# Softmax division moved behind the value product, with the sums broadcast by way of DRAM and the order laid out anew

## The chip, the cores and the metric

The kernel runs on one core of a Trainium2 chip. Its time is in device microseconds (us). A core has a matmul engine (PE, with its weight loads shown apart as PEld), a vector engine (DVE), an activation engine (ACT), a general engine (POOL, GpSimd) and a queue that only issues DMAs here (SP). Each takes its instructions in order; they wait for one another by semaphores. SBUF is the memory on the core, PSUM the matmuls' output memory (used here as two buffers of 128 x 1024 floats and four of 128 x 512), DRAM the memory outside.

## The reference

One transformer layer on x of shape (2, 1024, 512): attention with 16 heads of 32, then a feed-forward part with signs of weights, each followed by a residual and a layer norm. Everything is float32.

```python
qkv = jnp.einsum('bsd,ed->bse', x, w_qkv) + b_qkv          # (2, 1024, 1536)
q, k, v = ...                                              # (2, 16, 1024, 32)
scores = jnp.einsum('bhqd,bhkd->bhqk', q, k) / math.sqrt(Hd)
scores = scores + causal
attn = jax.nn.softmax(scores, axis=-1)
out = jnp.einsum('bhqk,bhkd->bhqd', attn, v)
...
x = layernorm(x + out @ w_out.T + b_out)
hidden = relu((x @ sign(up_weight).T) * up_scale)          # 2048 wide
x = layernorm(x + (hidden @ sign(down_weight).T) * down_scale * output_scale)
```

The softmax divides each row of exps by its sum. The sum depends on the query alone, so the division can be made on the probabilities or on the row of the value product.

## The kernel before

The attention runs in eight chunks: for each batch b (2) and each group e of four heads (4). A chunk has eight query tiles i of 128 rows; tile i needs the keys of i + 1 blocks of 128. For each chunk, `project` makes q, k and v of the four heads. To keep float32 accuracy in a faster matmul type, x and the weights are cut into forms (`prepare`: L585 truncates, L597 subtracts, L603 scales, L610 or L618 subtract again), and `matmuls` (L664) multiplies the forms. q and k are split once more (`split`, L746 and L751, on POOL) and written to DRAM and read back as "stacks", four loads for each (`stack`, DMAs of SP). x of batch 1 is loaded and cut in `load_x` (eight tiles), weights in `load_w` (three for a chunk).

`attend` handles a query tile. `scores` (L984, or L964 in the first half of the first chunk) makes scores of one, two or four heads in one of two double PSUM buffers ("d"). DVE adds the mask and takes the negated row maximum (L1021, or L1003 and L1013 where four heads go together), ACT takes the exp and sums each row (L1036, with the sums beside it in "small"). DVE takes the reciprocal of the sums (L1048), and POOL multiplies each row of probabilities by it (L1054, one instruction for each head). `transposes` (L1083) turns the probabilities block by block into a PSUM bank, and DVE or ACT copies them to SBUF (L547 is ACT's, L549 DVE's, `copied`). `values` (L1110) multiplies v by the turned probabilities; the result for a tile, four heads of 32 on the partitions and 128 queries along the row, is copied to "atT". When the last group of a batch is done, `output` (L1169) multiplies by the output weights, adds the residual and takes the layer norm's moments. The feed-forward part (L1296, L1340) runs at the end, from about 500 us on.

The order of the work is not that of the Python loops. Every step is a `Task` with a place (a number that grows with the work; one chunk is 36 units, as it has 36 blocks), the engines that may do it with a cost on each, and the tiles it reads and writes. `Plan.schedule` walks a clock of its own over these costs and gives, for each engine, the ripe task with the lowest place; where a task lists two engines, the one free first takes it. The result is a fixed order on each engine. Tiles have few slots, so a task can also wait for a buffer. A DMA counts as landed 2.3 units of that clock and its size over 200 GB/s after it is issued.

Lists at the top of the file shift places chunk by chunk: `LO` and `HI` bound the stretch over which the next chunk's projection is paced, `LOADW` and `PREPW` (and `LOADX`, `PREPX` for x of the second batch) say how far ahead of the chunk's base its weights are loaded and cut, `EAGER` how far the score matmuls go ahead, `FAST` the copies from PSUM, `BACK` the value product, `WAIT` the split of q and k, `TILES` the order of a chunk's query tiles, `TOGETHER` the tiles whose value product is held back and made with the next one, `ORDER` the order of the six products of a projection.

Probabilities live in a ring "pr" of four times 1024 columns, turned ones in "pt".

Of the kernel before, what the change touches and what calls it, by code (L numbers as in the profile page):

```python
# [11 lines left out]
F32R = mybir.dt.float32r  # L12
# [17 lines left out]

FAST = [8, 10, 8, 8, 8, 2, 8, 0]


TOGETHER = [(1, 3, 5), (1, 3, 5), (0, 1, 3, 5), (0, 3, 5), (0, 1, 3, 4, 6), (0, 1, 3), (0, 2, 4, 6), ()]
TILES = [[0, 1, 2, 3, 4, 5, 6, 7], [0, 1, 2, 3, 4, 5, 6, 7], [0, 1, 2, 3, 4, 5, 6, 7], [0, 1, 2, 3, 4, 5, 6, 7], [3, 2, 1, 0, 7, 6, 5, 4], [0, 1, 2, 4, 3, 5, 6, 7], [1, 2, 3, 0, 4, 5, 7, 6], [0, 1, 2, 3, 4, 5, 6, 7]]
HURRY = 6.0
# [3 lines left out]

HI = [0.9, 0.95, 0.95, 0.9, 0.8, 0.85, 0.95, 0.8]
LO = [0, -2, -4, 3, -1, -2, -2, -4]
LOADW = [15, 30, 30, 20, 5, 30, 30, 20]
LOADX = 10
PREPW = [2, 12, 10, 18, -6, 6, 18, 22]
PREPX = -5
BACK = [1, 1, 1, 4, 1, 9, 1, 1]
ORDER = [3, 0, 0, 0, 0, 0, 4, 4]
WAIT = [0, 8, -4, -2, 2, -2, 0, 4]
ONESX = (-6, 2, 4, 2)  # L50
# [8 lines left out]
SHARES = {'tp': 2, 'po': 1, 'f': 3, 'pu': 3, 'pb': 1}  # L59
EAGER = [25, 25, 20, 20, 20, 20, 20, 20]  # L60
WARM = 9
# [241 lines left out]
def kernel(  # L303
# [89 lines left out]
    def place_for(stack, name, n, kind=F32, side="left"):  # L393
# [5 lines left out]
    a_h = place_for(right, "split", 2 * 2 * TB, side="right")  # L399
    a_fl = place_for(right, "tmp", 3 * TB, side="right")  # L400
    a_v, a_wo, a_xb, a_at = (
        area("v", 2 * NQ * P), area("wout", NC * D), area("rows", 2 * D), area("atT", NC * S)
# [3 lines left out]
    def scratch(name, shape):  # L406
        return dram.tile(shape, F32, tag=name, name=name)

    d_x, d_w = scratch("dx", [NC, P, S]), scratch("dw", [NC, P, 3 * D])
    d_y = [scratch(f"dy{k}", [P, D]) for k in range(B * NQ)]  # L410
    d_h = [scratch(f"dh{k}", [2, P, TB]) for k in range(B * NC * 4)]
# [7 lines left out]

    a_pr, a_pt = place_for(left, "probs", 4 * 2 * TB), place_for(left, "probsT", PTB * P)  # L420

# [12 lines left out]
        "dy": d_y,  # L434
        "dh": d_h,
        "bqk": [bqk],
        "atT": views(a_at, (NC, P)),
# [58 lines left out]
    def of(t):  # L496
# [6 lines left out]
    rings = {  # L503
        "pr": (a_pr, 4 * 2 * TB // P), "pt": (a_pt, PTB)
    }
# [66 lines left out]

    latest = {}
    biases, dx, dw = new("bqk"), new("dx"), new("dw")

    def prepare(t, part, scaled, place, raw=None, parts=None):

        at = slice(None) if scaled else part
        flat = (lambda a: a.rearrange("p (a b) -> p a b", a=NC)) if scaled else (lambda a: a)
        form = lambda k: of(t)[:, k, at]  # L580
        T, given = new("tmp"), raw or (lambda: form(0).bitcast(F32))
        parts = parts or [t[0, part]]
        plan.task(
            dve(0.43),
            lambda _: nc.vector.tensor_scalar(  # L585
                flat(of(T)).bitcast(I32), given().bitcast(I32), -4096, None, ALU.bitwise_and
            ),
            place, parts, [T[0]], label="trunc",
        )
        if raw:  # L590
            plan.task(
                act(0.59), lambda _: nc.scalar.copy(form(0), flat(of(T))), place, [T[0]],
                [t[0, part]], label="high",
            )
        plan.task(
            either(0.69, 1.264),
            lambda e: engine[e].tensor_tensor(form(1), given(), flat(of(T)), ALU.subtract),  # L597
            place, [*parts, T[0]], [t[1, part]], label="low",
        )
        if scaled:  # L600
            plan.task(
                act(0.59),
                lambda _: nc.scalar.activation(  # L603
                    form(1), form(1).bitcast(F32), AF.Copy, scale=1 / U
                ),
                place, updates=[t[1, part]], label="scaled",
            )
            plan.task(
                either(0.69, 1.264),
                lambda e: engine[e].tensor_tensor(  # L610
                    form(2), flat(of(T)), form(1).bitcast(F32), ALU.subtract
                ),
                place, [T[0], t[1, part]], [t[2, part]], label="differ",
            )
        else:
            plan.task(
                dve(0.69),
                lambda _: nc.vector.scalar_tensor_tensor(  # L618
                    form(2), form(1).bitcast(F32), -1 / U, of(T), ALU.mult, ALU.add
                ),  # L620
                place, [T[0], t[1, part]], [t[2, part]], label="differ",
            )
# [119 lines left out]
    def split(hl, place, src=None, parts=()):  # L742

        hi, given = (lambda: of(hl)[:, 0]), src or (lambda: of(hl)[:, 1])
        plan.task(
            pool(0.61), lambda _: nc.gpsimd.tensor_copy(hi().bitcast(F32R), given()), place,  # L746
            parts or [hl[1]], [hl[0]], label="hi",
        )
        plan.task(
            pool(1.264),  # L750
            lambda _: nc.gpsimd.tensor_tensor(of(hl)[:, 1], given(), hi(), ALU.subtract),  # L751
            place, [*parts, hl[0]], updates=[hl[1]], label="lo",
        )
        return hl
# [31 lines left out]
    def project(b, e, lo, hi):  # L786

        v, got = new("v"), {}
        place = pace(lo, hi, 2 * (3 * 3 * NC + 2))
        for n, h in ORDERS[ORDER[b * NC + e]]:  # L790
            if n < 2:
                hl = split(product(b, e, n, h, place), place() - WAIT[b * NC + e])
                got[n, h] = stack(hl, n, place() - WAIT[b * NC + e])
            else:
                values_of(b, e, v, h, place)
        made[b, e] = got, v
# [152 lines left out]

    def scores(b, e, i, heads, at):  # L950
        G, N, W = len(heads), (i + 1) * P, 2 * TB // len(heads)
# [4 lines left out]

        sc, nm, sums = new("sc"), new("nm"), new("sums")
        pr = new("pr", blocks=G * (i + 1))
# [74 lines left out]
        for j in range(G):  # L1033
            marks[b, e, i] = plan.task(
                {"ACT": (0.25 + 0.852 * N / 1000, 0.37 + 0.852 * N / 1000)},
                lambda _, j=j: nc.scalar.activation(  # L1036
                    keys(of(pr), j, N),
                    keys(of(sc), j, W),
                    AF.Exp,
                    bias=of(nm)[:, j : j + 1],  # L1040
                    scale=sign,
                    accum_out=of(sums)[:, j : j + 1],
                ),
                at, [*[sc[1, k] for k in range(G)], nm[j]], [pr[j], sums[0]], label="exp",
            )
        plan.task(
            dve(0.16),
            lambda _: nc.vector.reciprocal(of(sums)[:, :G], of(sums)[:, :G]),  # L1048
            at - 50, updates=[sums[0]], label="recip",
        )  # L1050
        for j in range(G):
            plan.task(
                pool(0.254 + 0.843 * N / 1000),
                lambda _, j=j: nc.gpsimd.tensor_scalar(  # L1054
                    of(pr)[:, j * N : (j + 1) * N],
                    of(pr)[:, j * N : (j + 1) * N],
                    of(sums)[:, j : j + 1],
                    1.0,
                    ALU.mult,
                    ALU.mult,  # L1060
                ),
                at, [sums[0]], updates=[pr[j]], label="norm",
            )
# [34 lines left out]
    def values(b, e, some, at):  # L1098
# [27 lines left out]
        for n, (i, _) in enumerate(some):  # L1126
# [4 lines left out]
                at - FAST[b * NC + e], [to[0]], [rows[e]], label="at",  # L1131
            )

    waiting, marks = [], {}

    def attend(b, e, i, base, hold_back):

        units = grouped(i, 2 if (b, e) in plain and i < NQ // 2 else 4)
        each = []
        for n, heads in enumerate(units):  # L1140
            at = base + (i + 1) * n / len(units)
            pr = scores(b, e, i, heads, at)
            pt = transposes(i, heads, pr, at)
            each += [(u, pt, j * (i + 1)) for j, u in enumerate(heads)]
        waiting.append((i, each))
        if not hold_back:
# [7 lines left out]
    def output(b, i, place):  # L1154
# [7 lines left out]
        plan.task(  # L1162
            pool(1.264), lambda _: nc.gpsimd.tensor_tensor(of(xb), of(xb), bo, ALU.add), place(),
            [wout["bo"]], updates=[xb[0]], label="xb",
# [110 lines left out]
    def feed_forward(up, dn, dsc, base):  # L1275
        UNIT = 2.0

        def block(tb):
# [9 lines left out]
            for f in range(NFC):  # L1288
                pu, hf = new("pu"), new("hf", right_side)
                hh, hr = new("hh", ["pr", "pt"]), new("hr", ["pr", "pt"])  # L1290
                at = start + f * UNIT - (HURRY if final else 0)
# [139 lines left out]
    for at, (b, e) in enumerate(chunks):  # L1431
# [37 lines left out]
        if at + 1 == len(chunks):  # L1469
# [17 lines left out]
            for tb in range(1, NT // TB):  # L1487
                at0 = ff + (tb - 1) * NFC * 2.0
                load_rows(tb, at0 + 4)
                turn(tb, pace(at0 + 12, at0 + 28, 16), ["pr", "pt"])  # L1490
            feed_forward(up, dn, dsc, ff)
# [55 lines left out]
```

## Time and profile before

| | us |
|---|---|
| median of 3 runs (lowest, highest) | 761.28 (760.85, 761.53) |
| the profiled execution | 760.95 |
| its span, first to last instruction | 759.2 |
| PE busy | 735.4 |
| DVE busy | 533.3 |
| ACT busy | 415.5 |
| POOL busy | 333.0 |

The first two groups of the profile's costliest ones and the DMA queues (busy time and mean ns of one; packets, megabytes and share of 16 engines' span):

| group | |
|---|---|
| L1054 POOL, probabilities times reciprocal, x256 | 197.6 us, 782 ns |
| L1036 ACT, exp, x256 | 190.4 us, 754 ns |
| L1021 DVE, mask and maximum, x200 | 173.6 us, 876 ns |
| first DMA queue | 62,352 packets, 90.79 MB, 42.7% |
| second DMA queue | 1,232 packets, 0.53 MB, 0.2% |

A busy engine is one that has an instruction in flight. PE's matmuls overlap, so a busy PE need not be at its peak, but an idle one is lost time if PE sets the end. The profile can also be cut into stretches, which tells at what time each engine stood idle; and for each idle time it names the instruction that ended it. The granted clock is the share of full speed that PE was given in a stretch; it is 0.995 over the span.

### The profile page before, as it was taken

Reading aid. Unit: us, or ns where it says so; the run is one execution under the profiler, and the core shown is the slowest. Engines: PE = TensorE matmul, PEld = TensorE weight load, DVE = VectorE, ACT = ScalarE, POOL = GpSimd, SP = SyncE. Lnnn points to the kernel's source line nnn. Section 1 sums busy time; section 2 is a strip of 40 time slices with the busy share of each in tenths; the row PEclk is TensorE's granted clock in tenths of the full one; section 3 lists DMA queues with packets and bytes.
Section 4 is the critical chain, followed back from the end, with each engine's and each line's share of the span. In section 5 each row is a group of like instructions: output and inputs, shape, how many; then the busy total and the mean of one; then the engine's idle time right before and its main releaser. Section 6 shows DMA issues by size and latency. Waiting matters only on the chain.

```text
span 759.2 us, 15510 instructions
## 1 busy us (share of the span) xinstructions
PE 735.4 (97%) x5778; PEld 578.0 (76%) x5778; DVE 533.3 (70%) x1224; ACT 415.5 (55%) x934; POOL 333.0 (44%) x385
## 2 busy tenths in 40 slices
PE   9979999999879999999999999999999999999996
PEld 4657778888747777788888876667787777878885
DVE  5878977898998676697898789844337337335636
ACT  3637868788627467587788878734222222222210
POOL 2746675776874666567578565511001002001000
PEclk9999999999999999999999999999999999999998
DMA  7759965765716464474364384563003003000101
GB/s 218 174 137 274 241 200 141 164 186 132 200 71 152 136 158 132 106 194 132 94 154 137 90 266 140 175 210 113 1 0 111 1 0 112 1 0 1 56 0 57
DMA packets 63659, 92.32 MB, mean 122 GB/s; under 512 B 5088, under 2 KB 23648, under 8 KB 63584
## 3 DMA queue, kind: packets, MB, share of 16 engines
q1 hardware_dynamic: 62352, 90.79, 42.7%
q8 instruction: 46, 0.75, 0.4%
q10 hardware_dynamic: 1232, 0.53, 0.2%
q14 instruction: 29, 0.24, 0.1%
HBM read 66.66 MB, written 29.88 MB: 127 GB/s over the span
## 4 chain that ended last, share of the span: by engine, by line
PE 86%; DVE 9%; POOL 2%; issue 2%; ACT 1%; DMA 1%; ACTq 0%; DVEq 0%; POOLq 0%
PE s L1083 15%; PE s L1296 15%; PE pd L1340 14%; PE s L664 13%; PE d L984 9%; PE s L1110 8%; PE s L1169 7%; DVE d L1021 1%; DVE xforms L618 1%; POOL probs L1054 1%; PE s L914 1%; PE s L1245 1%; PE s L873 1%; PE s L705 1%; DVE small L1386 1%
## 5 line engine op out<-in xcount | busy, mean ns | idle before, releaser
L1054 POOL TENSOR_SCALAR probs<-probs,small 128x128 f32<-128x128 f32 (+7 forms) x256 | 197.6, 782 | 116.1 <-DVE small L1048 86.2
L1036 ACT ACTIVATE probs<-d,small 128x128 f32<-128x128 f32 (+7 forms) x256 | 190.4, 754 | 46.3 <-DVE small L1021 28.0
L1021 DVE CUSTOM_DVE_ANT_0 d<-d,mask 128x384 f32<-128x384 f32 (+7 forms) x200 | 173.6, 876 | 27.1 <-PE d L984 22.1
L1083 PE MATMUL s<-ident,probs 128*128 128x128 f32 x1152 | 169.0, 274 | 5.7 <-ACT probsT L547 2.4
L664 PE MATMUL s<-xforms,wforms 128*128 128x512 f32 x504 | 165.7, 431 | 2.0 <-DVE xforms L618 0.9
L1083 PEld LDWEIGHTS s<-ident,probs 128*128 128x128 f32 x1152 | 135.3, 141 | 37.7 <-issue 12.5
L1340 PE MATMUL pd<-stacks,hid 128*128 128x512 f32 (+1 forms) x512 | 132.9, 393 | 0.6 <-DVE hid L1313 0.6
L1296 PE MATMUL s<-xt,up 128*128 128x512 f32 x512 | 133.5, 400 | 0.0
L547 ACT COPY probsT<-s 128x512 f32<-128x512 f32 (+3 forms) x204 | 101.8, 528 | 52.8 <-PE s L1083 48.4
L1307 ACT ACTIVATE hf<-s,ups 128x512 f32<-128x512 f32 x64 | 44.0, 688 | 154.2 <-PE s L1296 146.5
L1313 DVE CAST hid<-hf 128x512 fp32r<-128x512 f32 x64 | 28.1, 438 | 124.7 <-ACT hf L1307 124.6
L984 PE MATMUL d<-stacks 128*128 128x512 f32 (+2 forms) x368 | 107.2, 382 | 6.1 <-ACT probs L1036 6.1
L1296 PEld LDWEIGHTS s<-xt,up 128*128 128x128 f32 x512 | 94.3, 188 | 23.8 <-issue 1.4
L1340 PEld LDWEIGHTS pd<-stacks,hid 128*128 128x128 f32 x512 | 92.9, 188 | 23.4 <-DVE hid L1313 1.5
L664 PEld LDWEIGHTS s<-xforms,wforms 128*128 128x128 f32 x504 | 87.0, 189 | 20.7 <-issue 6.1
L549 DVE COPY probsT<-s 128x512 f32<-128x512 f32 (+3 forms) x142 | 81.5, 582 | 14.2 <-PE s L1083 9.9
L1378 POOL TENSOR_TENSOR atT<-atT,back 128x512 f32<-128x512 f32 x9 | 12.9, 1449 | 166.5 <-issue 101.3
L984 PEld LDWEIGHTS d<-stacks 128*128 128x128 f32 x368 | 59.3, 190 | 27.0 <-ACT probs L1036 13.5
L1110 PE MATMUL s<-probsT,v 128*32 128x128 f32 x2304 | 72.1, 274 | 0.0
L1110 PEld LDWEIGHTS s<-probsT,v 128*32 128x32 f32 x2304 | 60.4, 110 | 14.6 <-issue 5.5
L1169 PE MATMUL s<-wout,atT 128*128 128x512 f32 x128 | 65.5, 603 | 0.0
L1036 ACT ACTIVATION_READ_ACCUMULATOR probs<-d,small 128x1 f32 x256 | 54.1, 211 | 0.0
(91 smaller groups left out, 671.0 us busy)
## 6 DMA issues: line engine op xcount, KB each, us to landing
stacks<-dh SPq DMA_DIRECT2D x124, 256.0 KB, 5.4
dh<-split SPq DMA_DIRECT2D x31, 512.0 KB, 3.3
wforms<-dw SPq DMA_DIRECT2D x18, 256.0 KB, 3.6
rows<-in_x SPq DMA_DIRECT2D x16, 256.0 KB, 4.4
dy<-rows SPq DMA_DIRECT2D x16, 256.0 KB, 2.2
raw<-in_up_wT SPq DMA_DIRECT2D x4, 1024.0 KB, 5.1
back<-dy SPq DMA_DIRECT2D x16, 256.0 KB, 4.6
out<-atT SPq DMA_DIRECT2D x16, 256.0 KB, 2.0
```

The source lines that it names most:

```text
L547: nc.scalar.copy(dst, src)
L549: nc.vector.tensor_copy(dst, src)
L664: lambda _, k=k, m=m, c=c: nc.tensor.matmul(bank(ps), lhsT=of(w)[:, m, c], rhs=of(x)[:, m, c], start=(k == 0), stop=(k + 1 == NC * len(for ...
L984: nc.tensor.matmul(of(sc)[:, at0 : at0 + n], lhsT=of(st[0, h])[:, u, ts(z, P)], rhs=of(st[1, g])[:, u, :n], start=True, stop=True,)
L1021: lambda _, j=j, some=some: nc.vector.tensor_tensor_reduce(some(), some(), keys(mask[:, S - N :], 0, N), scale=-1.0, scalar=LARGEST, op0=A ...
L1036: lambda _, j=j: nc.scalar.activation(keys(of(pr), j, N), keys(of(sc), j, W), AF.Exp, bias=of(nm)[:, j : j + 1], scale=sign, accum_out=of( ...
L1054: lambda _, j=j: nc.gpsimd.tensor_scalar(of(pr)[:, j * N : (j + 1) * N], of(pr)[:, j * N : (j + 1) * N], of(sums)[:, j : j + 1], 1.0, ALU. ...
L1083: lambda _, k=k, c=c, tp=tp: nc.tensor.transpose(of(tp)[:, k, :], of(pr)[:, c], ident),
L1110: nc.tensor.matmul(of(to)[ts(u, HD), n, :], lhsT=of(v)[:, k, ts(u, HD)], rhs=turned(pt, c + k, 1)[0], start=(k == i), stop=(k == 0),)
L1169: lambda _, c=c: nc.tensor.matmul(bank(py), lhsT=of(a)[:, c, :], rhs=of(wout)[:, c, :], start=(c == 0), stop=(c == NC - 1),),
L1296: lambda _, f=f, c=c, n=n, pu=pu: nc.tensor.matmul(of(pu), lhsT=of(up)[:, f // TPB, c, ts(f % TPB, P)], rhs=of(xt)[:, n, c, :], start=(c = ...
L1340: lambda _: nc.tensor.matmul(of(to)[:, d0:d1], lhsT=of(h)[:, ts(t, P)], rhs=of(dn)[:, f // 4, f % 4, d0:d1], start=(f == 0 and n == 0), st ...
```

## The change

The probabilities stay undivided through the transposes and the value product. One tile "sums" (128 queries by four heads) now serves all heads of a query tile; its reciprocal is taken once, written to DRAM as four rows of 128, and read back so that each of the four heads' 32 partitions holds its row of 128 reciprocals. POOL multiplies the tile of "atT" by that.

```diff
-        plan.task(
-            dve(0.16),
-            lambda _: nc.vector.reciprocal(of(sums)[:, :G], of(sums)[:, :G]),
-            at - 50, updates=[sums[0]], label="recip",
-        )
-        for j in range(G):
-            plan.task(
-                pool(0.254 + 0.843 * N / 1000),
-                lambda _, j=j: nc.gpsimd.tensor_scalar(
-                    of(pr)[:, j * N : (j + 1) * N],
...
-                at, [sums[0]], updates=[pr[j]], label="norm",
-            )
         return pr
...
                 at - FAST[b * NC + e], [to[0]], [rows[e]], label="at",
             )
+            plan.task(
+                pool(0.48),
+                lambda _, rows=rows, part=shares[b, e, i]: nc.gpsimd.tensor_tensor(
+                    of(rows)[:, e, :], of(rows)[:, e, :], of(part), ALU.mult
+                ),
+                at - FAST[b * NC + e], [shares[b, e, i][0]], updates=[rows[e]], label="share",
+            )
...
+        plan.task(
+            dve(0.16), lambda _: nc.vector.reciprocal(of(sums), of(sums)), at - 50,
+            updates=[sums[0]], label="recip",
+        )
+        line, shares[b, e, i] = new("dr"), new("rb")
+        dma(at - 40, lambda: of(line).rearrange("u q -> q u"), lambda: of(sums), 64,
+            [sums[0]], [line[0]], label="sums")
+        dma(
+            at - 40, lambda: of(shares[b, e, i]),
+            lambda: of(line).rearrange("(u o) q -> u o q", o=1).to_broadcast([NU, HD, P]), 64,
+            [line[0]], [shares[b, e, i][0]], label="shares",
+        )
```

Room for eight of these broadcast tiles ("rb") is taken from the probabilities' ring, which goes from four to three times 1024 columns; 64 small DRAM tiles ("dr") are new.

The costs that the planner uses for the cuts and splits change (for example truncation 0.43 to 0.60, subtraction on DVE 0.69 to 0.95 and on POOL 1.264 to 1.32). The lists of shifts change too, and one is new: `SKEW` shifts the three products of the second half of a projection to later places.

```diff
-FAST = [8, 10, 8, 8, 8, 2, 8, 0]
+FAST = [4, 8, 14, 8, 10, 8, 8, 6]
...
-LO = [0, -2, -4, 3, -1, -2, -2, -4]
-LOADW = [15, 30, 30, 20, 5, 30, 30, 20]
-LOADX = 10
-PREPW = [2, 12, 10, 18, -6, 6, 18, 22]
-PREPX = -5
-BACK = [1, 1, 1, 4, 1, 9, 1, 1]
-ORDER = [3, 0, 0, 0, 0, 0, 4, 4]
-WAIT = [0, 8, -4, -2, 2, -2, 0, 4]
...
+LO = [0, -3, 3, 13, -1, 1, 0, 13]
+LOADW = [30, 20, 10, 30, 15, 5, 15, 20]
+LOADX = 0
+PREPW = [0, 6, 10, 12, 8, 2, 0, 12]
+PREPX = 8
+SKEW = [16, 0, 0, 6, 0, 0, 4, 20]
+BACK = [0, 14, 1, 2, 14, 6, 0, 4]
+ORDER = [3, 0, 0, 0, 2, 0, 4, 4]
+WAIT = [8, -4, -4, 0, -2, -8, 2, -8]
...
+        whole, late = place, SKEW[b * NC + e]
         for n, h in ORDERS[ORDER[b * NC + e]]:
+            place = lambda units=0, h=h: whole(units) + h * late
```

`HI`, `TOGETHER`, `TILES` and `EAGER` change in the same way; the tile order 3, 2, 1, 0, 7, 6, 5, 4 goes from the fifth chunk to the fourth.

## The prediction

> **What bounds the kernel now.** I read the stretches first, then the waits, then the chain that ended last inside the worst stretch. Of the stretches (columns: microseconds from the span's start, length, then busy time and instruction count of PE, its weight loads, DVE, ACT and POOL, granted clock, DMA share, GB/s):
>
> ```profile
> 20.00:60.00 40.00, 35.05 (x266) 25.72 (x265) 31.85 (x62) 19.99 (x48) 23.37 (x24) 1.00 0.66 168
> 60.00:120.00 60.00, 57.51 (x607) 46.63 (x610) 51.82 (x131) 47.59 (x118) 41.62 (x51) 1.00 0.80 222
> 180.00:240.00 60.00, 53.26 (x514) 40.61 (x516) 55.14 (x119) 36.20 (x90) 44.39 (x46) 0.97 0.59 154
> 240.00:300.00 60.00, 60.00 (x511) 44.31 (x502) 43.46 (x99) 38.03 (x92) 38.15 (x43) 1.00 0.49 134
> 740.00:759.20 19.20, 12.90 (x67) 10.63 (x66) 12.69 (x31) 1.87 (x5) 0.00 (x0) 0.89 0.15 56
> ```
>
> PE is the bound: 735.4 of 759.2 us. Its 23.8 us of idle time stand in few places: 1.8 at the start, 4.95 in 20 to 60, 2.5 in 60 to 120, 6.7 in 180 to 240, 6.3 after the last matmul, and 1.6 in all the rest. So 14.2 us are open to a change of attention; from 240 on nothing is. In the worst stretch DVE is busy 55.14 of 60 us, and the clock falls to 0.97, which makes 53.26 us of PE work some 1.6 us longer. Open in all: 15.8 us.
>
> Who waits for whom (total, times, longest), of PE, its loads and POOL:
>
> ```profile
> PE d L984 <- ACT probs L1036: 6.1, 6, 3.6
> PE s L1083 <- POOL probs L1054: 1.4, 1, 1.4
> PEld s L1083 <- POOL probs L1054: 7.4, 19, 1.6
> POOL probs L1054 <- DVE small L1048: 86.2, 72, 4.2
> ```
>
> The transposes seldom wait for the normalising multiply on POOL (1.4 us that reached PE; 7.4 on loads, mostly under running matmuls). PE waits more for score buffers that the exps have not freed. The chain shows who made those late (start, length, what):
>
> ```profile
> 205.33 1.99 POOL probs L1054 x2
> ...
> 212.86 2.36 POOL xforms L597
> ...
> 215.24 1.28 DVE xforms L618
> ...
> 216.92 2.78 DVE xforms L618 x2
> ...
> 221.30 1.57 DVE xforms L597
> ```
>
> This is batch 1's x being cut into its forms (eight tiles, L585, L597, L618) in one burst on DVE and POOL, while the row maxima (L1021) and so the exps stand behind it in DVE's queue. DVE is slowed there, as the view of one line shows (min/median/max ns).
>
> ```profile
> L618 DVE SCALAR_TENSOR_TENSOR xforms<-xforms,tmp x16: 673/692/1767, 5.8 to 223.4; 128x512 fp32r<-128x512 f32 x16
> ```
>
> The same operation takes 673 or 1767 ns; POOL's instructions run beside the long ones.
>
> **Part by part.** Counts are those of the instructions in the two programs; PE has the same 4491, in another order, so its work does not change.
>
> *Removed on POOL:* 256 multiplies (L1054), 197.6 us. *Added on POOL:* 64 multiplies of 128x128 by the broadcast reciprocals. No such row exists: the nearest are the multiply by a column at 128x128 (0.388 us) and the two-tensor add at 128x512 (L1163, 1.305). Scaling the second by the first kind's ratio 0.388/0.804 gives 0.63, nearer the lower; 64 of them 40 us (25 to 84). Five "low" subtractions also come over from DVE, 5 x 1.3 = 6.5 us. POOL goes from 333 to about 182 us.
>
> *DVE:* 64 reciprocals instead of 178, 114 x 0.159 = 18.1 us less; 15 fewer 128x512 copies of transposed probabilities, 15 x 0.686 = 10.3 (ACT takes them, 15 x 0.591 = 8.9, inside its 45% idle); five fewer subtractions, 5 x 0.95 = 4.8. The lengthening beside POOL is, over L585, L597, L610 and L618, the busy time less count times shortest: 4.6 + 5.3 + 3.4 + 4.9 = 18.2 us; it could lose all or none, and as POOL's attention work halves I take 9. Together DVE loses 33 to 51, I take 42 of 533 us. Nothing of this is on PE's path by itself: it shortens what PE's 14.2 idle microseconds wait for.
>
> *Chain from exp to transposes:* a reciprocal (0.16) and a multiply (0.39 to 1.18) less. The matmuls of other work cover this today, so it is worth 1.4 us, and that lies inside the terms below.
>
> *Moved:* the split of batch 1's x is placed 13 units of the order earlier (PREPX -5 to 8) and the projection that needs it 10 later (LO of that chunk 3 to 13). Its eight loads on SP come 10 units later (LOADX 10 to 0, at the chunk's base), so the split can't start before the base, whatever its own place says. It started 2 units behind the projection's first place (base + 5 against base + 3) and now starts 13 ahead; 36 units are one chunk, some 62 us (eight chunks to about 500), so that is 22 us, as long as the burst took (202 to 224). In DVE's order the burst still stands as one, but tiles of chunk 3 now surround it. I take three quarters of 6.7 + 1.6 = 8.3, that is 6.3 us (bounds 0 and 8.3). For 20 to 120 us: POOL takes three of the first x subtractions before its first cast, and the third query/key split stands ahead of the first share multiply, where normalising multiplies of up to 2.48 us stood before it. Half of 7.45, 3.7 us (0 to 7.45).
>
> *New DMAs:* 64 writes of 128x4 sums by single elements (512 pieces each) and 64 broadcast reads, all on SP. Issue: the nearest rows are 0.43 us (stacks) and 0.62 (weights to scratch in 384 pieces), 64 x (0.62 + 0.43) = 67 us of a queue that waits most of the time. Landing is unknown: rows from 2.0 (out) to 6.1 (weights to scratch) each, 4 to 12 us for the pair. The reader is the share multiply, and behind it the output matmuls (L1169) of two chunks alone, 12 units (21 us) after their tile: that distance hides the pair. If it does not, POOL's splits queue behind a waiting share, then the stacks, then the next chunk's scores. Each read must also wait on SP for its write, and the stacks, weight and x loads stand behind it. Packets: 32,768 more, at 20 ns each (the second queue, 1232 in 0.2% of 16 engines' span) or 83 (the first, 62,352 in 42.7%): 5 to 21 us per engine for a 60 us chunk. The busiest such stretch uses 0.80, 48 us, and goes to 53, or to 69, which would not fit. I put 1.5 us on PE, near the lower end because only chunk 0 to 1 is that full; bounds 0 and 19 (first rival).
>
> The Trainium skill speaks against this part: "DMA: Bandwidth & Descriptors", section "Rules for kernel authors", says that a strided last dimension becomes one descriptor for each element and should be rearranged, and "Specifications" has writes under 512 B as read-modify-write. If that doubles the 20 ns row (an estimate from the page), the full stretch stands at 58 of 60 us and the sum stays as it is; no packet of such a write is in this trace.
>
> *Sum:* the profiled run took 760.95 us (span 759.2 and 1.75 around it). 760.95 - 6.3 - 3.7 + 1.5 = 752.45. The median of the runs shown is 0.33 above that run: **753 us**. All of the 15.8 and no new wait give 745.5; half of what I take off, with the 1.5, gives 757.8.
>
> **Rivals.** *The SP queue becomes the wait (slower).* For it: in chunk 0 the eight stacks loads were issued until 50.95 us, landing takes 5.4, and the first score from them starts at 57.0, so 0.65 us is all the slack. A write and a read of sums now stand between such loads. If a pair lands in 5.4 each rather than 2 to 3, loads go out up to 4.8 us late; with half covered by other matmuls, 2.4 at each of eight chunks, 19 us, less half my gain: 775. It decides from about 3 us a landing on. Against: later chunks stack long before their scores. *No net change:* DVE, which falls only from 410 to about 370 us in the first 500, still bursts, or the new order opens as many holes as it closes: 760 to 762. For it: the eight tiles of x still stand together in DVE's queue. *All holes close:* 746; for it, 240 to 360 runs with 0.15 us idle and the same kinds of work.
>
> **How the numbers follow.** Forecast 0.53, all holes 0.15, no net change 0.08, SP 0.24. A difference under 0.2% (1.5 us) can't be told from none here. Faster 0.68, same 0.08, slower 0.24. The forecast alone spans 746 to 758; reaching toward the SP case until 2 in 10 is left out, 744 to 770.
>
> **What would show it.** PE's idle time in the former 180 to 240 stretch under 2 us and the clock at 1.00 there; DVE near 490, POOL near 180; PE's busy time within 3 us of 735. L618's median stays, its maximum falls. Wrong would be: PE or its loads waiting for stacks from DRAM, SP's waits led by the sums' landing, or POOL splits behind the share multiply.

## The result, and the profile after

The changed kernel takes **948.37 us** (median of 4 runs, 943.79 to 950.82) where the kernel before takes 761.29 (760.85 to 761.53): 1.2451 times the time, 95% interval 1.2403 to 1.25. The forecast of 753, and its range up to 770, were wrong, in sign and by far in size.

From the page of the changed kernel: the span, the engines' busy time, the packets, the first DMA queue, the chain that ended last by engine and by line, and the groups of the transposes and of the new multiply (busy, mean ns, idle before it):

```profile
span 941.5 us, 15202 instructions
...
PE 788.4 (84%) x5778; PEld 616.3 (65%) x5778; DVE 516.9 (55%) x1089; ACT 425.0 (45%) x950; POOL 177.0 (19%) x198
...
DMA packets 105896, 96.61 MB, mean 103 GB/s; under 512 B 39136, under 2 KB 65888, under 8 KB 105824
...
q1 hardware_dynamic: 104592, 95.13, 53.3%
...
PE 53%; DMA 33%; DVE 5%; issue 4%; ACT 2%; SPq 2%; POOL 1%; another core or an unknown queue 0%; ACTq 0%; DVEq 0%; POOLq 0%
DMA dr<-small 13%; PE s L1304 12%; PE pd L1348 11%; PE s L1072 8%; PE s L669 6%; DMA dh<-split 6%; DMA wforms<-dw 5%; PE d L991 5%; DMA stacks<-dh 4%; PE s L1177 4%; PE s L1099 4%; SPq L572 2%; DMA dw<-in_w_qkvT 1%; DMA tmp<-in_w_qkvT 1%; DMA xforms<-dx 1%
...
L1072 PE MATMUL s<-ident,probs 128*128 128x128 f32 x1152 | 190.9, 297 | 65.0 <-ACT split L685 23.5
...
L1124 POOL TENSOR_TENSOR atT<-atT,shares 128x128 f32<-128x128 f32 x64 | 32.2, 509 | 273.6 <-DMA shares<-dr 174.4
```

And two lines of the page before, its chain by engine and its transposes:

```profile
PE 86%; DVE 9%; POOL 2%; issue 2%; ACT 1%; DMA 1%; ACTq 0%; DVEq 0%; POOLq 0%
...
L1083 PE MATMUL s<-ident,probs 128*128 128x128 f32 x1152 | 169.0, 274 | 5.7 <-ACT probsT L547 2.4
```

Read the chain first. Before, PE held 86% of it and DMAs 1%; now DMAs hold 33%. The largest of them is the write of the sums (dr<-small, 13%), but the next three are transfers that both kernels have: the split q and k on their way to DRAM (dh<-split), the weights' forms, the stacks. PE is busy 53.0 us longer with the same 5778 instructions, and idle 153.1 us (941.5 - 788.4) in place of 23.8; the two make the 182.3 us by which the span grew.

Stretches of the changed kernel (columns as in the prediction):

```profile
20.00:60.00 40.00, 27.53 (x195) 20.68 (x194) 14.32 (x34) 13.50 (x36) 8.22 (x10) 0.87 0.67 112
60.00:120.00 60.00, 47.64 (x411) 38.89 (x410) 45.71 (x83) 37.82 (x85) 20.69 (x19) 0.94 0.86 163
180.00:240.00 60.00, 49.61 (x455) 41.83 (x455) 35.31 (x80) 36.97 (x93) 13.18 (x16) 0.85 0.91 151
600.00:660.00 60.00, 39.71 (x270) 26.95 (x271) 27.06 (x65) 23.91 (x54) 8.17 (x10) 0.80 0.60 108
760.00:840.00 80.00, 79.65 (x353) 63.57 (x354) 38.85 (x80) 17.74 (x30) 4.30 (x3) 1.00 0.14 45
```

Every stretch of attention shown is slower; attention now ends near 690 us where it ended near 500. The feed-forward part (last line) runs as before, at full clock. In the stretches with large holes in PE the granted clock is lower, 0.80 in 600 to 660, and its matmuls take longer: the transposes' mean goes from 274 to 297 ns (L1072, the line that was L1083). In 60 to 120 the DMA engines are busy for 0.86 of the time and move 163 GB/s; before it was 0.80 and 222 GB/s. Busier engines that move less are the mark of this result.

Waits of the changed kernel (total, times, longest), first of SP's queue, then of the engines:

```profile
SPq L572 <- DMA dr<-small: 208.5, 48, 11.6
```

```profile
POOL atT L1124 <- DMA shares<-dr: 174.4, 28, 18.8
...
ACT split L685 <- DMA dh<-split: 53.2, 8, 12.5
...
PE d L991 <- DMA stacks<-dh: 27.8, 5, 15.2
...
PE s L1072 <- ACT split L685: 23.5, 5, 12.2
```

SP waits 208.5 us for the writes of the sums, as the list of signs at the end of the prediction had it for the case of being wrong; POOL's share multiply waits 174.4 us for the read, PE for late stacks.

The chain in a stretch of the first chunks (start, length, what), and SP's issues in a quiet stretch at the end of attention:

```profile
106.62 9.09 DMA wforms<-dw
...
120.37 15.84 DMA dh<-split
...
137.04 1.97 PE s L1072 x8
```

```profile
592.22 1.66 SPq L572 DMA_DIRECT2D dr<-small  x2
594.17 0.36 SPq L572 DMA_DIRECT2D dh<-split  x1
602.52 1.61 SPq L572 DMA_DIRECT2D shares<-dr  x2
604.23 0.42 SPq L572 DMA_DIRECT2D dr<-small  x1
604.76 1.64 SPq L572 DMA_DIRECT2D stacks<-dh  x3
614.87 0.54 SPq L572 DMA_DIRECT2D shares<-dr  x1
```

A read of the reciprocals waits on SP for its write, so the distance from the write's issue to the read's is the landing: 592.22 to 602.52, 604.23 to 614.87. A write of 2 KB in 512 single elements takes some **10.2 to 10.6 us**. Of the prediction's bounds for one landing, 2.0 and 6.1, the upper is exceeded by two thirds. The pair of writes at 592.22 landed together, so two of them do not take twice as long. And a write of split q and k, from a part of the kernel that the change leaves as it is, took 15.84 us. Before, the landings of such transfers were these (KB each, median us from issue to landing):

```profile
stacks<-dh SPq DMA_DIRECT2D x124, 256.0 KB, 5.4
dh<-split SPq DMA_DIRECT2D x31, 512.0 KB, 3.3
```

### The profile page after: what moved, and what is told of

It reads as the page before. It is cut to its first block, busy times and chain, and to the rows that moved or that the text cites. A ratio compares the mean times of both kernels' runs of the same rounds, so it can differ in the third digit from the quotient of the medians.

```text
span 941.5 us, 15202 instructions
## 1 busy us (share of the span) xinstructions
PE 788.4 (84%) x5778; PEld 616.3 (65%) x5778; DVE 516.9 (55%) x1089; ACT 425.0 (45%) x950; POOL 177.0 (19%) x198
## 4 chain that ended last, share of the span: by engine, by line
PE 53%; DMA 33%; DVE 5%; issue 4%; ACT 2%; SPq 2%; POOL 1%; another core or an unknown queue 0%; ACTq 0%; DVEq 0%; POOLq 0%
DMA dr<-small 13%; PE s L1304 12%; PE pd L1348 11%; PE s L1072 8%; PE s L669 6%; DMA dh<-split 6%; DMA wforms<-dw 5%; PE d L991 5%; DMA stacks<-dh 4%; PE s L1177 4%; PE s L1099 4%; SPq L572 2%; DMA dw<-in_w_qkvT 1%; DMA tmp<-in_w_qkvT 1%; DMA xforms<-dx 1%
## 5 line engine op out<-in xcount | busy, mean ns | idle before, releaser
L1072 PE MATMUL s<-ident,probs 128*128 128x128 f32 x1152 | 190.9, 297 | 65.0 <-ACT split L685 23.5
L1072 PEld LDWEIGHTS s<-ident,probs 128*128 128x128 f32 x1152 | 150.9, 153 | 105.7 <-ACT split L685 25.3
L669 PE MATMUL s<-xforms,wforms 128*128 128x512 f32 x504 | 185.0, 471 | 18.7 <-ACT split L685 10.2
L552 ACT COPY probsT<-s 128x512 f32<-128x512 f32 (+3 forms) x218 | 110.0, 529 | 104.3 <-PE s L1072 102.7
L669 PEld LDWEIGHTS s<-xforms,wforms 128*128 128x128 f32 x504 | 97.4, 211 | 41.4 <-ACT split L685 10.7
L991 PEld LDWEIGHTS d<-stacks 128*128 128x128 f32 x368 | 64.5, 205 | 69.2 <-issue 28.6
L554 DVE COPY probsT<-s 128x512 f32<-128x512 f32 (+3 forms) x128 | 72.4, 572 | 49.6 <-PE s L1072 45.8
L1124 POOL TENSOR_TENSOR atT<-atT,shares 128x128 f32<-128x128 f32 x64 | 32.2, 509 | 273.6 <-DMA shares<-dr 174.4
L1177 PE MATMUL s<-wout,atT 128*128 128x512 f32 x128 | 71.9, 659 | 4.1 <-POOL atT L1124 2.3
L685 ACT ACTIVATE split<-s,bqk 128x512 f32<-128x512 f32 x28 | 19.3, 690 | 68.3 <-DMA dh<-split 47.1
```

The lines of the kernel that those rows point to most:

```text
L552: nc.scalar.copy(dst, src)
L554: nc.vector.tensor_copy(dst, src)
L669: lambda _, k=k, m=m, c=c: nc.tensor.matmul(bank(ps), lhsT=of(w)[:, m, c], rhs=of(x)[:, m, c], start=(k == 0), stop=(k + 1 == NC * len(for ...
L991: nc.tensor.matmul(of(sc)[:, at0 : at0 + n], lhsT=of(st[0, h])[:, u, ts(z, P)], rhs=of(st[1, g])[:, u, :n], start=True, stop=True,)
L1072: lambda _, k=k, c=c, tp=tp: nc.tensor.transpose(of(tp)[:, k, :], of(pr)[:, c], ident),
L1177: lambda _, c=c: nc.tensor.matmul(bank(py), lhsT=of(a)[:, c, :], rhs=of(wout)[:, c, :], start=(c == 0), stop=(c == NC - 1),),
```

## The experiments

A run's before is the kernel before on the same chip (760.7 to 762.0 us).

### Without the two DMAs

```diff
+    nc.gpsimd.memset(a_rb, 1.0)
-        dma(at - 40, lambda: of(line).rearrange("u q -> q u"), lambda: of(sums), 64, ...)
-        dma(at - 40, lambda: of(shares[b, e, i]), lambda: of(line)...to_broadcast(...), 64, ...)
+        plan.task(DMA, lambda _: None, at - 40, [sums[0]], [line[0]], size=64, label="sums")
+        plan.task(DMA, lambda _: None, at - 40, [line[0]], [shares[b, e, i][0]], ...)
```

The write and the read are planned and not issued; POOL multiplies by ones, so nothing is divided. Expected:

> The changed kernel without its 128 new DMAs: the sums are neither written nor read, and POOL multiplies by ones, so the division is left out. Each compute engine has the changed kernel's order. Theory T (the 64 writes of 512 single elements hold the DMA engines some 10 us each, and everything from DRAM waits behind them): 745 to 757 us. Rival S (the DMA engines are free, but SP stands in order before each read until its write has landed): the same, 745 to 757. Rival O (the new order is what costs): above 880.

Measured 753.81 us (753.32 to 754.84), before 760.72: ratio 0.9908, interval 0.9885 to 0.9931. PE is busy 732.8 us, DVE 513.9, POOL 176.1. Its stretches:

```profile
20.00:60.00 40.00, 34.49 (x259) 25.76 (x258) 28.86 (x55) 20.53 (x49) 17.18 (x17) 0.96 0.75 194
60.00:120.00 60.00, 60.00 (x656) 51.74 (x655) 50.36 (x113) 52.48 (x129) 15.64 (x18) 1.00 0.76 193
...
180.00:240.00 60.00, 56.82 (x526) 43.05 (x524) 55.98 (x108) 43.19 (x100) 27.83 (x27) 0.97 0.57 148
```

PE, DVE and ACT run the same instructions in the same order as in the changed kernel. So the rest of the change is worth 6.9 us, and the two DMAs cost 194.6. The hole of 60 to 120 is closed (2.5 us idle before, 0 now), that of 180 to 240 half (6.7 to 3.2, with DVE still full and the clock still 0.97), that of 20 to 60 not (5.0 to 5.5). New holes of 2.8 us in all open in 120 to 180, 300 to 360 and 420 to 500, so PE's idle time falls by 3.6 us (23.8 to 20.2); its busy time falls by 2.6.

### The same bytes in fewer pieces

```diff
-        dma(at - 40, lambda: of(line).rearrange("u q -> q u"), lambda: of(sums), 64,
+        dma(at - 40, lambda: of(line).rearrange("u q -> (u q)").rearrange("(q u) -> q u", u=NU), lambda: of(sums), 64,
```

The tile is written as it stands, 128 pieces of 16 B; each head's partitions then read 128 reciprocals that are not theirs. In the second kernel it is written in 256 pieces of 8 B (pairs of heads; places again not theirs). All else is the changed kernel.

> The changed kernel, but the sums go to DRAM row by row, 128 pieces of 16 bytes instead of 512 of 4; the read is the same, so POOL multiplies by reciprocals in the wrong places. Same order, same bytes, same waits. T (time goes with the number of pieces, 8 on each engine instead of 32): a landing of 2 to 4 us and 755 to 800 us. Fixed landing time of any small write to DRAM: above 900. O: above 900.

> The same with 256 pieces of 8 bytes, 16 on each engine. T: landing about 5 us, between the 128-piece and the 512-piece kernel, 790 to 870 us. Fixed landing time: above 900.

Measured (one run each): **756.95** us with 128 pieces, **777.63** with 256, against 948 with 512. The second is below its expected 790 to 870. SP's issues, first of the kernel with 256 pieces, then of that with 128:

```profile
455.20 0.42 SPq L572 DMA_DIRECT2D dr<-small  x1
456.54 1.28 SPq L572 DMA_DIRECT2D stacks<-dh  x3
460.19 0.54 SPq L572 DMA_DIRECT2D shares<-dr  x1
```

```profile
440.49 0.32 SPq L572 DMA_DIRECT2D dr<-small  x1
440.91 2.11 SPq L572 DMA_DIRECT2D stacks<-dh  x3
443.83 0.54 SPq L572 DMA_DIRECT2D shares<-dr  x1
```

The landing is 5.0 us with 256 pieces and 3.3 with 128; SP waits for such writes 58.6 us in all (longest 5.4) and 15.3 (longest 3.0). PE, DVE and ACT have the same order in the kernel with 128 pieces as in the one without DMAs, and it is 3.1 us slower: a round trip through DRAM for each tile is nearly free. With the bytes the same, the cost goes with the count of pieces.

### Is it SP, standing before the read?

```diff
-            lambda: of(line).rearrange("(u o) q -> u o q", o=1).to_broadcast([NU, HD, P]), 64,
+            lambda: x[:NU, :P].rearrange("(u o) q -> u o q", o=1).to_broadcast([NU, HD, P]), 64,
```

The write stays, but the read takes rows of x, and so waits for no write; the factors are then entries of x.

> The changed kernel with its 512-piece writes, but the broadcast reads take four rows of x, so that no read waits for a write (POOL multiplies by the wrong values). Same order on every compute engine. T: the writes still hold the DMA engines and SP's eight DMA semaphores, 880 to 950 us. S: 750 to 790.

Measured 947.12 us (one run), the same as with the wait. Two of SP's waits in this kernel:

```profile
SPq L572 <- DMA dh<-split: 62.5, 16, 9.0
...
SPq L572 <- DMA dr<-small: 40.1, 15, 5.2
```

SP's wait for the sums falls from 208.5 us to 40.1 and nothing is won. The transfers themselves are slow: its wait for split q and k grows from 26.0 to 62.5 us, and POOL still waits 161.7 us for the reads, which wait for no write. (SP's DMAs share eight semaphores in turn, so SP can also stand until an older DMA has landed; the waits for the sums that are left are probably of this kind.) The longest line in the list of waits was not the cause by itself.

### What the writes cost by themselves

Three kernels (one run each). First, the kernel *before* with the 64 writes added, of columns of the identity, into DRAM tiles that nobody reads:

```diff
+        line = new("dr")
+        dma(base + i - 39, lambda: of(line).rearrange("u q -> q u"), lambda: ident[:, :NU], 64,
+            writes=[line[0]], label="sums", after=[marks[b, e, i]])
```

Then the changed kernel with the writes alone (no reads, POOL multiplies by ones), and with writes and reads where POOL multiplies by the identity and so waits for no read; in both nothing is divided.

> The kernel before, with its own division and lists, and 64 writes of 512 single elements from a constant tile to DRAM beside it, one for each query tile, which nobody reads or waits for. T: the writes alone fill the DMA engines for 64 x 10 us: 880 to 960 us. S: SP has nothing behind them to wait for, 762 to 775. O: 762 to 775.

> The changed kernel with its writes of 512 pieces but without the reads; POOL multiplies by ones (the division is left out). Same order on every engine. It parts the 88 us between the kernel before with such writes (859) and the changed one (948). If the new lists leave less room for late loads: 930 to 950. If the broadcast reads behind the writes, and POOL standing at them, make the rest: 850 to 880.

> The changed kernel with its writes and its reads, but POOL multiplies by a constant tile, so it waits for no read (the division is left out). If POOL standing in order at the share multiply holds up the splits behind it: 850 to 890. If only the DMA engines count: 930 to 950.

Measured 858.91, 887.12 and 928.87 us; the first is below its expected 880 to 960, the second between its two cases. So in the changed order: 753.8 without DMAs, 133 more for the writes, 42 more for the reads, 19 more for POOL's wait at the share multiply (the changed kernel's own runs lie up to 7 us apart). In the order of before, the writes alone cost 97 us (762.04 to 858.91), though nothing reads them. A stretch, two of SP's waits and the first DMA queue of that kernel, and the first of these waits in the kernel before:

```profile
60.00:120.00 60.00, 48.76 (x451) 39.51 (x450) 42.25 (x103) 36.70 (x90) 33.04 (x39) 0.94 0.98 167
```

```profile
SPq L569 <- DMA dh<-split: 94.6, 22, 9.6
...
SPq L569 <- DMA dr<-ident: 23.9, 13, 3.4
```

```profile
q1 hardware_dynamic: 96144, 90.93, 55.0%
```

```profile
SPq L567 <- DMA dh<-split: 32.1, 15, 4.0
```

The DMA engines are busy 0.98 of this stretch and move 167 GB/s; without the writes it was 0.80 and 222. SP's wait for split q and k to land was 32.1 us with a longest of 4.0 before, and is 94.6 with 9.6 here.

The landings themselves can be read from the traces: a DMA has landed at the last update of its semaphore ahead of that semaphore's next use. For the kernel before this gives the 5.4 and 3.3 us of its page. Medians in us:

| kernel | stacks, 256 KB | split q and k, 512 KB | write of the sums |
|---|---|---|---|
| before | 5.4 | 3.3 | none |
| changed, without the two DMAs | 5.6 | 3.2 | none |
| changed, 16 pieces (below) | 5.3 | 3.5 | 1.8 |
| changed, 128 pieces | 5.5 | 4.1 | 3.3 |
| changed, 256 pieces | 6.7 | 6.1 | 5.9 |
| changed, 512 pieces | 8.7 | 10.1 | 10.7 |
| before, with 64 writes of 512 | 9.0 | 9.0 | 11.8 |

A landing is counted from the issue, so what SP waits ahead of it is not in these figures. The transfers that both kernels share, unchanged in bytes and pieces, take up to three times as long to land beside the writes of 512 pieces. This is the mechanism: **the writes hold up the other transfers in the DMA engines, and the loads that PE lives on land late.** How much of the 97 us goes by way of SP, which waits 23.9 us for these writes themselves though nobody reads them, was not separated.

### The lists and costs without the moved division

The division of before (reciprocals and 256 multiplies on POOL), with the new lists and planner costs. No diff is shown, as it is the lists of the change put into the kernel before.

> The kernel before with its division ahead of the transposes, but the changed kernel's lists and planner costs. It parts the 7 us that the changed kernel gains without its DMAs: if they come from the new lists, 752 to 757 us; if from the freed POOL and DVE, 760 to 775, as the lists were laid for a free POOL.

Measured 763.11 us (762.49 to 765.59), before 762.04: ratio 1.0021, interval 1.0011 to 1.0032. The new lists gain nothing by themselves: 60 to 120 has 4.0 us idle and 180 to 240 has 5.5. The 6.9 us belong to the division moved together with the lists laid out for it; the moved division with the old lists was not run.

### Other ways to the turned reciprocals

The turn from 128 x 4 to 4 x 128 can be made on the core. First on PE, without DRAM: POOL spreads the reciprocals over 128 columns, PE turns them, DVE or ACT copies them back.

```diff
-        dma(at - 40, lambda: of(line).rearrange("u q -> q u"), lambda: of(sums), 64, ...)
-        dma(at - 40, lambda: of(shares[b, e, i]), ...)
...
+        plan.task(pool(0.42), lambda _: nc.gpsimd.tensor_copy(of(wide).rearrange("p (u r) -> p u r", u=NU),
+            of(sums)[:, :, None].to_broadcast([P, NU, HD])), at - 40, [sums[0]], [wide[0]], label="shares")
+        plan.task(TURN, lambda _: nc.tensor.transpose(of(tp)[:, 0, :], of(wide), ident), at, ...)
+        plan.task(copy(P), lambda g: copied(g, of(wide), of(tp)[:, 0, :]), at, ...)
```

> The division stays behind the value product, but the reciprocals don't go by DRAM: POOL spreads the 128x4 tile to 128x128, PE turns it (64 more transposes at 0.109 us, 7 us of PE), and DVE or ACT copies it back to SBUF (64 copies at 0.28 us, 18 us shared). T: 754 plus 7, less what idle time takes: 756 to 764 us, and no wait of SP for small writes. If DVE or ACT becomes the bound by the copies: 765 to 775.

Measured 777.07 us (776.87 to 777.79), ratio 1.0198 (1.0181 to 1.0215), above what was expected. PE is busy 748.1 us, 15 more than without the DMAs, and has holes that the kernel without the DMAs has not: busy 52.76 of 60 us in 180 to 240 (there 56.82) and 73.83 of 80 in 420 to 500 (78.84). Why they open was not followed up.

Second, no turn at all: 16-byte pieces, every partition reads all 512 reciprocals of the tile, and POOL multiplies in four parts of 32 partitions, each with its head's column. The larger tile leaves room for two in place of eight.

```diff
-    a_rb = place_for(left, "shares", 8 * P)
+    a_rb = place_for(left, "shares", 2 * NU * P)
...
-                    of(rows)[:, e, :], of(rows)[:, e, :], of(part), ALU.mult
+                        of(rows)[ts(u, HD), e, :], of(rows)[ts(u, HD), e, :],
+                        of(part)[ts(u, HD), :, u], ALU.mult,
...
+        dma(at - 40, lambda: of(line), lambda: of(sums), 64, [sums[0]], [line[0]], label="sums")
...
-            lambda: of(line).rearrange("(u o) q -> u o q", o=1).to_broadcast([NU, HD, P]), 64,
+            lambda: of(line).rearrange("(o q) u -> o (q u)", o=1).to_broadcast([P, P * NU]), 256,
```

> The division behind the value product by way of DRAM, without small pieces where it hurts: the sums are written as 128 pieces of 16 bytes, every partition reads all 512 reciprocals (2 KB in one piece), and POOL multiplies in four instructions of 32 partitions, each taking every fourth reciprocal. Two slots for the broadcast tiles instead of eight. T: 757 of the 16-byte kernel, and POOL some 110 us busier, off the path: 756 to 763 us. If two slots or POOL's queue hold it up: 765 to 790.

Measured 790.7 us (789.12 to 792.06), ratio 1.038 (1.0361 to 1.0399), the second case expected and just above its range. The multiplies are now 256 of 539 ns, 137.4 us: a quarter of the partitions, with every fourth reciprocal read, costs as much as all of them (509 in the changed kernel). SP waits 61.1 us for them to free one of the two tiles. Which weighs more, the two tiles or POOL's longer work, was not separated.

Third, DVE turns 32 x 32 blocks. With the reciprocals spread 32 times along the row, row 32g of the result holds, for all heads, the 32 queries of block g: four rows, written in 16 pieces of 128 B to the places that the changed kernel uses. Read and multiply are those of the change.

```diff
+        wide = shares[b, e, i]
+        plan.task(dve(0.3), lambda _: nc.vector.transpose(of(wide),
+            of(sums)[:, :, None].to_broadcast([P, NU, HD])), at - 50, [sums[0]], [wide[0]], label="turn")
-        dma(at - 40, lambda: of(line).rearrange("u q -> q u"), lambda: of(sums), 64,
+        dma(at - 40, lambda: of(line).rearrange("u (g q) -> g u q", q=HD),
+            lambda: of(wide)[0:P:HD, :].rearrange("g (u q) -> g u q", u=NU), 64,
...
```

> The reciprocals are spread over 128 columns and turned in 32x32 blocks by one DVE instruction (64 more on DVE), so that the write to DRAM has 16 pieces of 128 B in place of 512 of 4 B; the broadcast read and the multiply on POOL stay. Theory (what costs is the count of pieces, some 0.02 us each of landing, and engine time taken from other DMAs): the read is issued about 3 us after the write, as with 128 pieces of 16 B, SP waits for the write under 20 us in all, and the time is that of the kernel without the two DMAs, 753.8, plus up to 6 for the 64 DVE instructions (64 x 0.1 to 0.3 us = 6 to 19 us of DVE, which has slack outside the stretches where it sets the pace): 753 to 761, ratio 0.99 to 1.00. Rival A (a round trip through DRAM costs what it costs, whatever its pieces): the pair still takes 10 us and the time is above 850. Rival B (any step more in the chain opens new holes in the planned order, as the turn on PE did): SP waits little, PE's busy time as in the kernel without the DMAs (733), yet idle time in the stretches 180 to 240 and 420 to 500 us, and 765 to 780.

Measured **762.64** us (761.27 to 766.19; 10 runs), before 761.89: ratio 1.0012, interval 0.9998 to 1.0026, where the changed kernel has 1.2451; this is just above the theory's 753 to 761 and 0.99 to 1.00. SP's issues of this kernel, and its new group on DVE:

```profile
251.32 0.54 SPq L572 DMA_DIRECT2D dr<-shares  x1
252.05 0.34 SPq L572 DMA_DIRECT2D dy<-rows  x1
252.94 0.52 SPq L572 DMA_DIRECT2D shares<-dr  x1
```

```profile
L1149 DVE STREAM_TRANSPOSE shares<-small 128x128 f32<-128x128 f32 x64 | 19.7, 307 | 2.5 <-issue 0.4
```

The landing is 1.6 us, and SP waits 8.5 us for all 64 writes. The time is 186 us below the changed kernel's, of the 194.6 that the two DMAs cost. It is 8.8 above the kernel without the DMAs (1.2 of it is that this chip runs the kernel before slower), in PE's order (463 of the program's 4491 PE instructions stand elsewhere), in the 64 turns, or in both. The last kernel tells the planner 0.1 us for the turn and places it at the end of its tile; 176 instructions of PE then stand elsewhere.

```diff
-            dve(0.3),
+            dve(0.1),
-            at - 50, [sums[0]], [wide[0]], label="turn",
+            at + 2, [sums[0]], [wide[0]], label="turn",
```

> As the kernel with the turn on DVE, with the turn told to the planner as 0.1 us in place of 0.3 and placed at the tile's end in place of 50 units ahead of it. PE's order then agrees in 4315 of 4491 instructions with that of the kernel without the DMAs (4028 before); the work is the same. Theory (what is left between 762.6 and 753.8 is the order, not the 64 turns): PE's idle time falls from 24.9 to some 20 to 22 us and the time to 754 to 759, ratio 0.990 to 0.997. Rival (the turns themselves, 64 x 0.307 = 19.7 us of DVE, cost it): 760 to 765, ratio 0.998 to 1.004.

Measured **759.26** us (758.0 to 760.21; 6 runs), before 761.46: ratio 0.9966, interval 0.9954 to 0.9978, just above the theory's range of 754 to 759 and its ratio inside it. This one is 0.3% faster than the kernel before and computes all that it does. Its PE and a stretch:

```profile
PE 734.2 (97%) x5778; PEld 580.7 (77%) x5778; DVE 528.5 (70%) x1153; ACT 420.3 (55%) x947; POOL 178.9 (24%) x200
```

```profile
60.00:120.00 60.00, 59.91 (x655) 51.62 (x654) 51.53 (x121) 51.83 (x126) 15.70 (x18) 1.00 0.67 178
```

60 to 120 is closed again, for 57.06 with the turn placed early. But PE's idle time is 24.2 us (758.4 - 734.2) where the theory had 20 to 22: it fell by 0.7 from 24.9, while PE's busy time fell by 2.6 (736.8 to 734.2). So the theory's time nearly came and its way did not. How much of the remaining 5.4 us is the turns' 19.6 us of DVE and how much is order stays open.

## Why the prediction was wrong

**The step that failed: the new DMAs, +1.5 us (bounds 0 and 19); measured +194.6.** It went wrong in two places.

*The landing* was bounded "from 2.0 (out) to 6.1 (weights to scratch)", and it is 10.2. The upper row was a write in 384 pieces, and the new one has 512: scaled by pieces, 6.1 x 512 / 384 = 8.1. The prediction named the pieces when it costed the issue, and not when it bounded the landing. The list it took its rows from also held landings of 8.5 to 10.7 us.

*The packets* were priced by their own recorded time, 20 to 83 ns each, 5 to 21 us per engine and chunk. A packet of 4 B is recorded with less than that, 9 ns in the median. What the price left at nothing is what such a write does to the transfers beside it. The packets of 2 KB, as many in both kernels, took 115 ns each in the mean before, and none over 1.6 us; with 64 writes added to the kernel before they took 151 ns, the longest 6.2 us, and in the changed kernel 162 and 7.2. Added up, the 64 landings of that kernel with writes are 772 us; they overlap, and at least one write was in flight for 495 of its first 601 us, so nearly all of attention ran beside one.

The prediction asked whether a distance of 21 us hides the latency of the pair. That part was the smaller one: freeing the multiply of its wait gave back 19 us. What no distance hides is the time that stacks, splits and weights lose in the DMA engines.

**The rival on SP was right in sign, not in its mechanism.** It had 775 us at 5.4 us a landing, deciding from about 3 on; 256 pieces (5.0 us) gave 778, which is luck as far as the mechanism goes, and 128 pieces (3.3 us) gave 757 and so nothing slower. It put the cost on loads queued behind a waiting read, and taking that wait away in the changed kernel won nothing (947). It was given 0.24, and its own price stopped inside the landing's bounds.

**The gains, -6.3 and -3.7, together 10.0; measured 6.9.** Without the DMAs the hole in 60 to 120 closes and that in 180 to 240 by half, and the 6.1 us that PE waited for score buffers are no longer among its waits; but DVE is still the full engine in 180 to 240 (55.98 of 60 us) and the clock stays at 0.97, not 1.00. The stretch of 20 to 60 gave nothing; the "up to 2.48 us" of a normalising multiply there is a line of two, and the longest single one is 1.65. DVE was to lose 42 us and lost 19 (533 to 514), outside its bounds of 33 to 51. The lengthening beside POOL, of which half was to go, is still there, 18 us by the same reckoning: the subtraction that was L618 has a median of 894 ns for 692 and still reaches 1751, where its maximum was to fall. And the reciprocals, counted at 18.1 us, mostly lay over other instructions' records: DVE's busy time before is 533.3 us with them and 524.5 without.

**What held.** POOL near 182 (177.0), the share multiply at 25 to 84 us with 40 taken (32.2; 509 ns for the 630 estimated), the issue on SP (0.42 for the write, 0.54 for the read), ACT 9 us more (425.0 for 415.5). PE within 3 us of 735 holds without the DMAs (732.8), not with them: the falling clock was on no list.

**The rule that the prediction weighed.** The Trainium skill's page "DMA: Bandwidth & Descriptors" says under "Rules for kernel authors" that a strided last dimension becomes one descriptor for each element. The traces agree: with the 64 writes added to the kernel before, its first queue has 33,792 packets more (62,352 to 96,144), 528 of 4 B for each write of 512 elements. It was the right warning, priced with the wrong row. The same section warns against a turn by a plain DMA's access pattern, and puts it 19 times behind the chip's own DMA transpose; "VectorE: DVE Perf Modes", section "The three transpose paths", says the same for a large innermost destination stride. No run here has that transpose; 512 pieces landed 6 times later than 16. That second section also has DVE's turn of 128 x 128 by 32 x 32 blocks at 311 ns in bf16; the row here, in float32, is 307. As to the page's read-modify-write under 512 B ("Specifications" of the first page), pieces of 128 B landed in 1.6 us, so being under 512 B alone is not what costs.

## What to carry to other kernels

Count the pieces of a new DMA before its bytes, and cost it twice: as a latency for its reader, and as delay of the other transfers, the loads that feed the bound engine above all. When the profile has a write with many pieces, take its landing as a starting point and scale it up by the count of pieces, not as an upper bound. A turn of a small tile belongs on an engine with slack (here one DVE instruction of 0.307 us in place of 496 pieces), and after any such edit the planned order has to be laid out again, as one step moved the time by 3 us with its place and its planned cost alone.

## What the hardware showed beyond that

- Writes to DRAM of 2 KB landed after 1.6 us in 16 pieces (128 B), 3.3 in 128 (16 B), 5.0 in 256 (8 B) and 10.2 in 512 (4 B) in the places shown; the medians of all 64 are 1.8, 3.3, 5.9 and 10.7. The first kind updates its semaphore five times and the others 16 times in most writes, which suggests that it runs on fewer DMA engines; so it differs from them in more than the pieces.
- The delay is not recorded at the small packets. With the 64 writes added to the kernel before, the first queue went from 42.7% of 759.2 us to 55.0% of 857.1, which is 147 us more per engine. Packets of 4 B hold 30 of these; the other 117 are packets of 512 B and 2 KB, as many as before, that took longer. A stretch's DMA share near 1 beside falling GB/s (0.98 and 167 after 0.80 and 222) was the better sign.
- Holes in PE came with a lower clock: beside 129.3 us more of idle time the stretches shown up to 660 us have a granted clock of 0.80 to 0.94, and the same matmuls were busy 53.0 us longer.
- POOL took 539 ns to multiply 32 partitions by 128, one operand read at every fourth element, and 509 for 128 partitions by 128 without that step.
